# Row vectors sent as lines, tables written by halves, and a first norm centred ahead of the ranks, in a two-layer graph attention kernel

## The chip, the cores and the metric

The kernel runs on one core of a Trainium2 chip. The metric is the device time of one execution in microseconds, the median of three runs. Before the change it is 2462.87 us (2462.56 to 2469.74); the profiled execution took 2464.5 us.

The engines are named as in the profile: PE is the matrix engine (TensorE), PEld its weight loads, DVE is VectorE, ACT is ScalarE, POOL is GpSimd, and SP is SyncE, which issues most DMA transfers. "POOLq" and "SPq" are the instruction queues of GpSimd and SyncE.

## What is computed

The input is x, 16 batches of 1024 nodes with 256 features, and one adjacency matrix of 1024 x 1024. Two residual layers follow one another, all in fp32:

```
# layer 0
h   = relu(layernorm(x))
r   = relu(h @ mlp1_w + b1)                     # 1024 x 512
a   = elu(gat(r, None, W_fc, a_fc))             # dense attention, slope 0.2
o   = elu(a) + r
r2  = relu(o @ mlp2_w + b2)                     # 1024 x 256
b   = elu(gat(r2, adj, W_hand, a_hand))         # masked attention, slope 0.2
x   = x + relu(elu(b) + r2)
# layer 1
h   = relu(layernorm(x))
g   = h @ W
x   = x + relu(softmax(mask(leaky(e_src + e_dst, 0.01))) @ g)   # masked by adj

def gat(inp, adj, W, a):
    h = inp @ W;  f1 = h @ a[:F];  f2 = h @ a[F:]
    e = leaky_relu(f1[:, None] + f2[None, :]);  mask by adj if given
    return elu(softmax(e) @ h)
```

## The kernel before

The work of one batch is spread over two and more steps of a software pipeline. In one step, which lasts some 147 us, the kernel does the masked attention of layer 0 of batch b, the masked attention of layer 1 of the batch before, the dense attention of batch b + 1 or b + 2, and the first norm of a batch still later. The names are: `Norm` (layer norm and transposition to features by nodes), `Dense` (first MLP, dense attention, second MLP), `Gnn0` and `Gnn1` (masked attentions; `Masked` is their base).

**The dense attention is not done as a 1024 x 1024 product.** leaky_relu makes the weight of a pair one of two products, according to the sign of f1 + f2. So the nodes are sorted by f2, running sums over the sorted rows are kept from both ends, and each node looks up the two sums at its own threshold. The steps are:

- `project` (L453) makes h on PE, with f1 and f2 as extra columns; ACT copies it to SBUF as `hnat`.
- `columns` (L468) gathers f2 of the 8 tiles in `fs` on DVE. `send` (L473) writes these 1024 numbers to DRAM (`row_r`), through the helper `send_row` (L240); `row` (L476) reads them back, broadcast to 128 partitions (`r`, 512 KB).
- `rank` (L501) counts, for a tile of 128 nodes, how many nodes come before each, in 3 or 4 passes of DVE over the broadcast row. `sign` (L540) counts on ACT against the other threshold.
- `scatter` (L518) writes the rows of a tile to their sorted place in DRAM by an indirect DMA; `read_sorted` (L555) reads the sorted rows back as `xs`, 8 consecutive rows to a partition, in two halves.
- `sums_weights` (L584) makes `bd` on ACT; `sum_before` (L591) makes the running sums `tt` from the front, and `sum_behind` (L608) those from the end, in place in `xs`, on DVE. `write_table` (L599) writes `tt` and `xs` to the table `fine` in DRAM, 2 MB each. `carry` (L617) makes the sums between partitions on PE and writes them to the table `coarse`.
- `gather` (L628) reads, for each tile, one row of `fine`, and adds one of `coarse`, by indirect DMA on GpSimd. `share`, `mean`, `merge` and `merge_end` (L643 to L719) put the result together, transpose it (`hpT` on PE) and add it to `resT`; `mlp2` (L721) follows.

**The first norm** of a batch (`first_norm`, L774) takes statistics (L258, L259 on DVE), a root on GpSimd (L263, L264), centres (L268 on DVE, `hn`) and transposes on PE (L278, `nt`), four tiles at a time; ACT applies the relu (L282, `hT`). It does this for half 0 and, some 20 us later, for half 1.

**The masked attention of layer 1** needs a row of weights broadcast as well (`rowsb`). It goes the same way, through `send_row`, as `row_b` and back (L349 to L360).

**The order of work is written out by hand.** `at(lo, hi, steps)` puts steps in a table with a time in us, and at the end the table is sorted and emitted in that order. For PE, DVE, ACT and SP this order is the order of instructions on the engine, and GpSimd is chained to it likewise, apart from the scatters, which are free among themselves. The times only sort: each engine works its queue in order and waits for what an instruction needs. `t0` is the start of a step; a period is written as 142.

A transfer on SP waits for its data at the head of SP's queue. The tiles of x come from one pool of three buffers with the tag `x`: `load_first` (L753) fetches x for the first norm, `load_again` (L756) fetches it once more for the residual sums.

The change touches `send_row` and its two callers, `write_table`, and the times of `first_norm`, `dense_begin` (L798), `dense_sums` (L813), `load_again` in `masked_first` (L863), `m.send` in `second_norm` (L902), `load_first` (L1022), and the table writes of the written-out start (L960, L962, L992, L994).

Of the kernel before, what the change touches and what calls it, by code (L numbers as in the profile page):

```python
# [8 lines left out]
F32 = mybir.dt.float32  # L9
# [8 lines left out]
P = 128  # L18
# [13 lines left out]
def fast_path(ctx: ExitStack, tc: tile.TileContext, alarm, x, adj, w1, b1, w2, b2, w_fc, a_fc,  # L32
# [21 lines left out]
    nc = tc.nc  # L54
    NB, N, F = x.shape
    H = w1.shape[1]
    NT = N // P
# [5 lines left out]
    K = H + 1  # L63
# [3 lines left out]
    work = ctx.enter_context(tc.tile_pool(name="work", bufs=2))  # L67
# [10 lines left out]
    def bc_psum(name):  # L78
        return psum.tile([P, NH * HALF], F32, tag="bc", name=name, bufs=1)
# [11 lines left out]
    ident = const.tile([P, P], F32, name="ident")  # L91
# [90 lines left out]
    row_d = {s: [dram.tile([1, N], F32, name=f"row_{s}{k}") for k in range(2)] for s in "rb"}  # L182
# [39 lines left out]
    def at(lo, hi, steps):  # L222
        for i, step in enumerate(steps):
            table.append((lo + (hi - lo) * i / len(steps), len(table), step))
# [12 lines left out]
        for u in range(len(col)):  # L237
            nc.tensor.transpose(dst[:, u * P:(u + 1) * P], col[u].to_broadcast([P, P]), ident)

    def send_row(dst, col):  # L240

        nc.sync.dma_start(dst.rearrange("o (u i) -> i (o u)", i=P), col)

    class Norm:

# [46 lines left out]
    def half(h):  # L292
        return slice(h * TH, (h + 1) * TH)
# [4 lines left out]
    class Masked:  # L298
# [48 lines left out]
            nc.vector.tensor_scalar_max(qwd[:, 2, :], qwd[:, 2, :], D_MIN)  # L347

        def send(self):  # L349
            send_row(row_d["b"][self.b % 2], self.qwd[:, 0, :])  # L350

        def row(self, sent=False):

# [74 lines left out]
    class Dense:  # L428
# [42 lines left out]
            nc.vector.tensor_reduce(self.ext, self.fs[:, 1, :], AX.X, OP.max)  # L471

        def send(self):  # L473
            send_row(row_d["r"][self.b % 2], self.fs[:, 1, :])

        def row(self, sent=False):  # L476

# [77 lines left out]
        def read_sorted(self):  # L555

            if self.split:
                self.xs = [big.tile([P, TH, R], F32, tag=tag, name=f"xs_{self.b}_{h}", bufs=bufs)
                           for h, (tag, bufs) in enumerate((("onat", 1), ("x", 3)))]
            else:  # L560
                xs = big.tile([P, NT, R], F32, tag="seq", name=f"xs_{self.b}", bufs=2)
                self.xs = [xs[:, half(h), :] for h in range(2)]
                self.xs_all = xs
            rows = sorted_d[self.b % 2].rearrange("(p r) f -> p r f", p=P)
            for h in range(2):
                reader = nc.sync.dma_start(self.xs[h], rows[:, half(h)])
                for made in self.writers:
                    wait_for(reader, made, "rows of the buffer")
                self.readers.append(reader)

        def sums_begin(self):
            b = self.b
            self.bd = small.tile([P, 2, NT], F32, tag="bd", name=f"bd_{b}")
            if self.split:
                self.tt = [big.tile([P, TH, K], F32, tag="hm", name=f"tt_{b}_{h}", bufs=2)
                           for h in range(2)]
            else:
                tt = big.tile([P, NT, K], F32, tag="seq", name=f"tt_{b}", bufs=2)
                self.tt = [tt[:, half(h), :] for h in range(2)]
                self.tt_all = tt  # L580
            self.all_t = work.tile([P, K], F32, tag="part", name=f"all_{b}")
            nc.gpsimd.memset(self.tt[0][:, 0, :], 0.0)

# [12 lines left out]
            else:  # L596
                nc.vector.scalar_tensor_tensor(tt[r + 1], row, bd, tt[r], op0=OP.mult, op1=OP.add)

        def write_table(self, s):  # L599

            dst = fine_d[self.b % 2][:N, s * K:(s + 1) * K].rearrange("(p r) f -> p r f", p=P)
            if self.split:
                for h, part in enumerate(self.xs if s else self.tt):
                    nc.sync.dma_start(dst[:, half(h)], part[:, :, :K])
            else:
                nc.sync.dma_start(dst, self.xs_all[:, :, :K] if s else self.tt_all)

        def sum_behind(self, r):  # L608
            rows = [self.xs[u // TH][:, u % TH, :K] for u in range(NT)]
# [140 lines left out]
    xs = {}  # L750
# [17 lines left out]
    def each(f, *ranges):  # L768
        out = [()]
        for r in ranges:  # L770
            out = [o + (i,) for o in out for i in r]
        return [partial(f, *o) for o in out]

    def first_norm(t0, b):  # L774

        n = norm1[b]
        lo = t0 - (62 if b == 2 else 29.5)
        at(lo, lo + 1, n.stats_steps(0))
        at(t0 - 13, t0 - 9, n.stats_steps(1))
        n.turn_at(t0 - (14.5 if b == 2 else 22), 0, 4)  # L780
        n.turn_at(t0 + 0.2, 1, 4)

    def mlp_steps(b):
# [13 lines left out]

    def dense_begin(t0, b):  # L798
        d = dense[b]
        at(t0 - 38.5, t0 - 38.5, [d.columns, d.send, partial(d.row, True)])  # L800
        at(t0 - 31.5, t0 - 31.5, [d.highest])
        at(t0 - 28, t0 - 12, each(d.rank, range(NT)))
        at(t0 - 33, t0 - 30.5, [partial(d.project, t, 0) for t in range(2)])
        at(t0 - 21, t0 - 8, [partial(d.project, t, 0) for t in range(2, NT)])
        scatters(d, t0 - 18.5, t0 - 4.5)
        at(t0 - 6, t0 - 6, [d.query])
        at(t0 - 4, t0 - 4, [d.read_sorted])
# [5 lines left out]
    def dense_sums(t0, b):  # L813
        d = dense[b]
        at(t0 - 3, t0 - 3, [d.sums_begin])
        at(t0 - 22, t0 - 4, each(d.sign, range(NT)))
        for h in range(2):
            at(t0 + 6.5 + 4 * h, t0 + 6.5 + 4 * h, [partial(d.sums_weights, h)])
            at(t0 + 7.5 + 5 * h, t0 + 12.5 + 5 * h, each(d.sum_before, tiles(h)))
        at(t0 + 18, t0 + 18, [partial(d.write_table, 0)])  # L820
        at(t0 + 18, t0 + 32, each(d.sum_behind, range(NT - 1, -1, -1)))
        at(t0 + 32, t0 + 32, [partial(d.write_table, 1)])
        at(t0 + 33, t0 + 33, [d.count])
        at(t0 + 50.5, t0 + 50.5, each(d.carry, range(2)))

# [31 lines left out]
    def masked_first(t0, b):  # L857
        m, n = gnn0[b], norm2[b]
        at(t0 + 1, t0 + 1, [m.vectors])
        at(t0 + 4, t0 + 4, [m.row])  # L860
        at(t0 + 4.5, t0 + 10, each(m.scale, range(NT)))
        weights(m, 0, t0 + 5.5, t0 + 10)
        at(t0 + 3, t0 + 3, [partial(load_again, b)])  # L863
        at(t0 + 4.5, t0 + 11, each(dense[b].natural, range(NT // 2)))
        at(t0 + 11, t0 + 39, each(m.product, range(NQ), range(NT)))
        for q in range(1, NQ):
            weights(m, q, t0 + 5.5 + 7 * q, t0 + 12 + 7 * q)
        for t in range(NT):
            lo = t0 + 18.2 + 7 * (t // 2) + 0.6 * (t % 2)
            at(lo, lo, [partial(m.finish, t)])  # L870
            at(lo + 1.2, lo + 1.2, [lambda t=t: m.combine(t, dense[b].o_nat)])
            at(lo + 5.2, lo + 5.2, [lambda t=t: m.update(t, xs[b])])
            at(lo + (6.2 if last(b) or b == 0 else 9), lo + (6.2 if last(b) or b == 0 else 9), [partial(n.stats, t)])
        at(t0 + 36, t0 + 36, [partial(n.root, 0)])
        lo = t0 + (46.5 if last(b) or b == 0 else 51)
        at(lo, lo, [partial(n.root, 1)])
# [4 lines left out]
    def second_norm(t0, b):  # L881
        n, m = norm2[b], gnn1[b]
        if last(b):
            n.turn_at(t0 + 46.5, 0)
            n.turn_at(t0 + 49, 1, 1.6)
            lo = t0 + 50
        elif b == 0:
            n.turn_at(t0 + 47, 0)
            n.turn_at(t0 + 50.5, 1, 1.6)
            lo = t0 + 47.2  # L890
        else:
            n.turn_at(t0 + 53.3, 0)
            n.turn_at(t0 + 67.3, 1)
            lo = t0 + 71
        at(lo, lo + 7, each(m.project, range(NT)))
        at(lo + 7.5, lo + 7.5, [m.extremes])
        if last(b, 2):
            at(lo + 7.8, lo + 7.8, [m.vectors])
            at(lo + 8.2, lo + 8.2, [m.row])
            at(lo + 8.3, lo + 9.5, each(m.scale, range(NT)))  # L900
        else:
            at(lo + 11, lo + 11, [m.vectors, m.send])  # L902
            at(lo + 40, lo + 52, each(m.scale, range(NT)))
            at(base_of(b + 1) + 22, base_of(b + 1) + 22, [partial(m.row, True)])

# [51 lines left out]
    for h in range(2):  # L957
        at(START + 82 + 3 * h, START + 82 + 3 * h, [partial(d.sums_weights, h)])
        at(START + 83 + 4 * h, START + 87 + 4 * h, each(d.sum_before, tiles(h)))
    at(START + 91, START + 91, [partial(d.write_table, 0)])  # L960
    at(START + 91, START + 98, each(d.sum_behind, range(NT - 1, -1, -1)))
    at(START + 98, START + 98, [partial(d.write_table, 1)])  # L962
    at(START + 98, START + 98, [d.count])
    at(START + 100, START + 100, each(d.carry, range(2)))
    for t in range(TH):
# [23 lines left out]
    for h in range(2):  # L989
        at(START + 150 + 3 * h, START + 150 + 3 * h, [partial(e.sums_weights, h)])  # L990
        at(START + 151 + 5 * h, START + 156 + 5 * h, each(e.sum_before, tiles(h)))
    at(START + 161, START + 161, [partial(e.write_table, 0)])  # L992
    at(START + 161, START + 175, each(e.sum_behind, range(NT - 1, -1, -1)))
    at(START + 175, START + 175, [partial(e.write_table, 1)])  # L994
    at(START + 175, START + 175, [e.count])
    at(START + 180, START + 180, each(e.carry, range(2)))
    for b in range(NB):
# [21 lines left out]
            dense_rows(after_base - PERIOD, b + 2)  # L1019
            dense_begin(after_base, b + 2)  # L1020
        if b + 3 < NB:
            lo = after_base - PERIOD + 73  # L1022
            at(lo, lo, [partial(load_first, b + 3)])
            first_norm(after_base, b + 3)

# [464 lines left out]
```

## Time and profile before

| engine | busy us | share of the span |
|---|---|---|
| PE | 2305.0 | 94% |
| PEld (beside PE) | 1779.3 | 72% |
| DVE | 1635.6 | 66% |
| ACT | 1252.3 | 51% |
| POOL | 967.2 | 39% |

The page gives busy time of each engine, groups of instructions with the idle time ahead of them, and what ended that idle time. A group's line is read from the left: line of the kernel, engine, operation, what it writes and reads, shape, count; then busy us and mean ns; then us of idle time of that engine just ahead of it, with the releaser. The timeline lists an engine's instructions in order of time: start, length, engine, line, operation, and in brackets the idle time ahead. The chain of waits goes from the last instruction backwards to what released it; a piece of it with "DMA" is a transfer on which the next instruction waited.

DMA moves 348.41 MB in the span, 141 GB/s on the average. By tenths of the span's slices its engines are busy from 2 to 8, so it comes in bursts. In the stretch from 1000 to 1150 us its share of busy time is 1.01 to 1.07 from 1110 to 1140 us and 0.01 from 1000 to 1010 us.

### The profile page before, as it was taken

To read this page: it belongs to the slowest core of one execution; us is meant where nothing else is said; L and a number is where in the kernel's file an instruction comes from. 1 tells how busy PE (TensorE), PEld (TensorE's weight loads), DVE (VectorE), ACT (ScalarE), POOL (GpSimd) and SP (SyncE) were. 2 spreads that over 40 slices of the span, in tenths; PEclk is the share of its full clock that TensorE was granted. 3 is DMA by queue.
4 is the path that set the end of the run, shared out by engine and by line. 5 is a ranking of instruction groups with operands and counts; after the bars stand their busy time and mean duration, and the time that the engine had idled before them with its cause. 6 is when DMAs were issued, how large, how long until landed. Compare 5 with 4: busy or idle time off the path is not lost.

```text
span 2464.5 us, 30883 instructions
## 1 busy us (share of the span) xinstructions
PE 2305.0 (94%) x10025; PEld 1779.3 (72%) x10025; DVE 1635.6 (66%) x4499; ACT 1252.3 (51%) x2712; POOL 967.2 (39%) x1216
## 2 busy tenths in 40 slices
PE   8988899998999999999899989989999999999897
PEld 6666677776867768677776867767676786877666
DVE  6765684765847567684765857567684865858554
ACT  4355645546455553645546355553645546364442
POOL 1153344253433526344353523526344353533320
PEclk9999999999999999999999999999999999999899
DMA  4558266482645728256482645638266482736600
GB/s 171 154 161 203 52 163 159 137 213 68 191 103 158 185 100 206 76 165 158 136 214 93 176 92 163 180 112 201 74 177 148 129 214 94 187 87 165 161 1 28
DMA packets 176714, 348.41 MB, mean 141 GB/s; under 512 B 39192, under 2 KB 90392, under 8 KB 172448
## 3 DMA queue, kind: packets, MB, share of 16 engines
q1 hardware_dynamic: 130592, 182.36, 27.7%
q0 software_dynamic: 45952, 163.99, 24.7%
q8 instruction: 82, 1.34, 0.3%
q14 instruction: 88, 0.72, 0.1%
HBM read 220.06 MB, written 126.24 MB: 141 GB/s over the span
## 4 chain that ended last, share of the span: by engine, by line
PE 57%; DVE 20%; DMA 13%; ACT 4%; POOL 3%; issue 2%; DVEq 0%; POOLq 0%; ACTq 0%; SPq 0%
PE h L461 16%; PE oa L380 9%; PE ob L380 7%; PE m L447 7%; DMA row_r<-fs 6%; PE pa L318 4%; DVE attb L369 4%; DVE atta L369 4%; PE pb L318 3%; DMA got<-coarse,k 3%; POOL got L637 3%; PE m L726 3%; DMA r<-row_r 3%; PE nt L278 3%; DVE xs L614 2%
## 5 line engine op out<-in xcount | busy, mean ns | idle before, releaser
L461 PE MATMUL h<-wfc_sb,resT 128*128 128x257 f32 x2048 | 477.8, 388 | 0.0
L380 PE MATMUL oa<-hma,atta 128*128 128x258 f32 x2048 | 457.4, 383 | 11.4 <-DVE atta L369 11.4
L380 PE MATMUL ob<-hmb,attb 128*128 128x257 f32 x2048 | 456.5, 382 | 5.5 <-DVE attb L369 5.5
L380 PEld LDWEIGHTS oa<-hma,atta 128*128 128x128 f32 x2048 | 385.6, 190 | 78.3 <-DVE atta L369 22.8
L380 PEld LDWEIGHTS ob<-hmb,attb 128*128 128x128 f32 x2048 | 389.9, 191 | 61.0 <-ACT hmb L364 3.7
L461 PEld LDWEIGHTS h<-wfc_sb,resT 128*128 128x128 f32 x2048 | 391.0, 195 | 56.1 <-issue 1.0
L719 POOL TENSOR_TENSOR resT<-resT,e 128x512 f32<-128x512 f32 x128 | 163.1, 1274 | 410.7 <-DVE e L718 365.6
L369 DVE SCALAR_TENSOR_TENSOR atta<-rowsa,qwda,edge 128x256 f32<-128x256 f32 x512 | 263.3, 542 | 47.3 <-ACT rowsa L360 33.0
L404 POOL TENSOR_TENSOR posa<-posa,onat 128x256 f32<-128x256 f32 x120 | 106.7, 889 | 437.8 <-ACT posa L396 437.8
L369 DVE SCALAR_TENSOR_TENSOR attb<-rowsb,qwdb,edge 128x256 f32<-128x256 f32 x512 | 256.6, 530 | 29.1 <-PE ob L380 26.4
L447 PE MATMUL m<-hT,w_sb 128*128 128x512 f32 x512 | 235.8, 598 | 0.5 <-ACT posa L396 0.5
L726 PE MATMUL m<-resT,w_sb 128*128 128x512 f32 x512 | 230.3, 596 | 4.4 <-POOL resT L719 4.4
L395 ACT ACTIVATE ea<-oa,reca 128x256 f32<-128x256 f32 x128 | 60.8, 475 | 330.5 <-DVE reca L392 304.3
L637 POOL DMA_INDIRECT got<-coarse,k x124 | 194.6, 1569 | 38.1 <-issue 36.9
L418 ACT ACTIVATE rb<-ob,recb 128x256 f32<-128x256 f32 x128 | 57.5, 474 | 267.0 <-DVE recb L416 267.0
L278 PE MATMUL nt<-ident,hn 128*128 128x128 f32 x512 | 86.9, 318 | 101.1 <-DVE hn L268 98.0
L710 DVE TENSOR_SCALAR e<-hpT 128x512 f32<-128x512 f32 x128 | 88.3, 690 | 139.9 <-PE hpT L708 135.3
L726 PEld LDWEIGHTS m<-resT,w_sb 128*128 128x128 f32 x512 | 93.9, 191 | 106.9 <-issue 94.1
L637 POOL DMA_INDIRECT got<-fine,k x124 | 129.7, 1046 | 78.8 <-DVE ea L405 35.6
L278 PEld LDWEIGHTS nt<-ident,hn 128*128 128x128 f32 x512 | 69.4, 162 | 124.5 <-issue 89.8
L509 DVE TENSOR_SCALAR_CACHE_REDUCE junk<-r,fs 128x1024 uint8<-128x1024 f32 (+7 forms) x128 | 103.5, 809 | 83.4 <-DMA r<-row_r 82.6
L447 PEld LDWEIGHTS m<-hT,w_sb 128*128 128x128 f32 x512 | 92.6, 193 | 88.8 <-issue 86.1
(177 smaller groups left out, 3592.7 us busy)
## 6 DMA issues: line engine op xcount, KB each, us to landing
xs<-sorted SPq DMA_DIRECT2D x32, 1028.0 KB
fine<-tt SPq DMA_DIRECT2D x15, 2052.0 KB
fine<-xs SPq DMA_DIRECT2D x15, 2052.0 KB
x<-in_x_dram SPq DMA_DIRECT2D x16, 1024.0 KB
out_dram<-x SPq DMA_DIRECT2D x32, 512.0 KB
xn<-in_x_dram SPq DMA_DIRECT2D x15, 1024.0 KB
coarse<-carry SPq DMA_DIRECT2D x32, 256.5 KB
r<-row_r SPq DMA_DIRECT2D x14, 512.0 KB
```

The lines of the kernel that those rows point to most:

```text
L278: nc.tensor.transpose(self.ps[c][:, u * P:(u + 1) * P], self.hn[t][:, c * P:(c + 1) * P], ident)
L318: nc.tensor.matmul(ps[:, :2 + F], lhsT=hT[:, c, t * P:(t + 1) * P], rhs=self.w_sb[:, c, 0, :], start=(c == 0), stop=(c == FC - 1))
L369: nc.vector.scalar_tensor_tensor(a_t, self.rows[:, q * PAIR:(q + 1) * PAIR], self.qwd[:, 1, j:j + 1], edge[:, j, q * PAIR:(q + 1) * PAIR], ...
L380: nc.tensor.matmul(self.out[t][:, :F + self.ONES], lhsT=self.att[q, j][:, (t % 2) * P:(t % 2 + 1) * P], rhs=self.hm[:, j, 2:2 + F + self.O ...
L404: adder.tensor_add(pos, pos, o_nat[:, t, :])
L447: nc.tensor.matmul(ps, lhsT=w1_sb[:, kc, c * P:(c + 1) * P], rhs=hT[:, kc, h * HALF:(h + 1) * HALF], start=(kc == 0), stop=(kc == FC - 1))
L461: nc.tensor.matmul(ps[:, :F + 1], lhsT=self.resT[:, kc, t * P:(t + 1) * P], rhs=wfc_sb[:, kc, g, :], start=(kc == 0), stop=(kc == HC - 1))
L509: nc.vector.tensor_scalar(junk[:, t * P:], r2[:, t * P:], s, None, op0=OP.is_lt, op1=OP.add, accum_out=rank[:, 1, t:t + 1])
L637: nc.gpsimd.indirect_dma_start(out=got[u // n][:, u % n, :], out_offset=None, in_=(coarse_d if coarse else fine_d)[self.b % 2][:, :], in_o ...
L710: nc.vector.tensor_scalar_min(e, ps, 0.0)
L719: nc.gpsimd.tensor_add(dst, dst, e)
L726: nc.tensor.matmul(ps, lhsT=w2_sb[:, kc, c * P:(c + 1) * P], rhs=self.resT[:, kc, h * HALF:(h + 1) * HALF], start=(kc == 0), stop=(kc == H ...
```

## The change

It has five parts.

1. A row of 1024 numbers, which lies in SBUF as 128 partitions x 8, is transposed on PE to 8 partitions x 128 and copied by ACT to a tile `line`, and goes to DRAM as 8 lines of 128 numbers. Before, the DMA wrote it as 1024 single numbers. The column copy keeps its time, the send comes 1.7 later in the table; the send of the weights of layer 1 comes 13 later.
2. In the steps from the fourth batch on, the statistics of the first norm come 4 earlier in the table and its first centring 3 earlier, which puts the statistics ahead of `highest` and three of four centrings ahead of the first rank. The fourth comes after it.
3. The tables `fine` are written in two halves each, and each half as soon as its sums are there: the sums from the front write half 0 first, the sums from the end half 1 first.
4. `load_again` comes 7 later and `load_first` 13 later in the table, meant to keep them out of the way of rows and gathers.
5. The start is changed accordingly.

```diff
-    def send_row(dst, col):
-
-        nc.sync.dma_start(dst.rearrange("o (u i) -> i (o u)", i=P), col)
+    def send_row(dst, col, name):
+
+        ps = bc_psum(f"{name}_ps")
+        nc.tensor.transpose(ps[:NT, :P], col, ident)
+        line = work.tile([NT, P], F32, tag="carry", name=name, bufs=2)
+        nc.scalar.copy(line, ps[:NT, :P])
+        nc.sync.dma_start(dst.rearrange("o (u i) -> (o u) i", i=P), line)
...
-        def write_table(self, s):
+        def write_table(self, s, h):
 
             dst = fine_d[self.b % 2][:N, s * K:(s + 1) * K].rearrange("(p r) f -> p r f", p=P)
-            if self.split:
-                for h, part in enumerate(self.xs if s else self.tt):
-                    nc.sync.dma_start(dst[:, half(h)], part[:, :, :K])
-            else:
-                nc.sync.dma_start(dst, self.xs_all[:, :, :K] if s else self.tt_all)
+            nc.sync.dma_start(dst[:, half(h)], (self.xs if s else self.tt)[h][:, :, :K])
...
     def first_norm(t0, b):
 
         n = norm1[b]
-        lo = t0 - (62 if b == 2 else 29.5)
+        lo = t0 - (62 if b == 2 else 33.5)
         at(lo, lo + 1, n.stats_steps(0))
         at(t0 - 13, t0 - 9, n.stats_steps(1))
-        n.turn_at(t0 - (14.5 if b == 2 else 22), 0, 4)
+        n.turn_at(t0 - (14.5 if b == 2 else 22), 0, 4 if b == 2 else 7)
         n.turn_at(t0 + 0.2, 1, 4)
...
-        at(t0 - 38.5, t0 - 38.5, [d.columns, d.send, partial(d.row, True)])
+        at(t0 - 38.5, t0 - 38.5, [d.columns])
+        at(t0 - 36.8, t0 - 36.8, [d.send, partial(d.row, True)])
...
-        at(t0 + 18, t0 + 18, [partial(d.write_table, 0)])
+        at(t0 + 13, t0 + 13, [partial(d.write_table, 0, 0)])
+        at(t0 + 18, t0 + 18, [partial(d.write_table, 0, 1)])
         at(t0 + 18, t0 + 32, each(d.sum_behind, range(NT - 1, -1, -1)))
-        at(t0 + 32, t0 + 32, [partial(d.write_table, 1)])
+        at(t0 + 25, t0 + 25, [partial(d.write_table, 1, 1)])
+        at(t0 + 32, t0 + 32, [partial(d.write_table, 1, 0)])
...
-        at(t0 + 3, t0 + 3, [partial(load_again, b)])
+        at(t0 + 10, t0 + 10, [partial(load_again, b)])
...
-            at(lo + 11, lo + 11, [m.vectors, m.send])
+            at(lo + 11, lo + 11, [m.vectors])
+            at(lo + 24, lo + 24, [m.send])
...
-    at(START + 98, START + 98, [partial(d.write_table, 1)])
+    at(START + 98, START + 98, each(d.write_table, [1], (1, 0)))
...
-    at(START + 175, START + 175, [partial(e.write_table, 1)])
+    at(START + 168, START + 168, [partial(e.write_table, 1, 1)])
+    at(START + 175, START + 175, [partial(e.write_table, 1, 0)])
...
-            lo = after_base - PERIOD + 73
+            lo = after_base - PERIOD + 86
             at(lo, lo, [partial(load_first, b + 3)])
```

## The prediction

> **What bounds the kernel now.** I read the page's busy shares first: PE is busy 94% of the span, DVE 66%, so the question is where PE's missing 6% lies. The list of waits gives one large answer, and the costliest groups say the same on two lines:
>
> ```profile
> L278 PE MATMUL nt<-ident,hn 128*128 128x128 f32 x512 | 86.9, 318 | 101.1 <-DVE hn L268 98.0
> ...
> L509 DVE TENSOR_SCALAR_CACHE_REDUCE junk<-r,fs 128x1024 uint8<-128x1024 f32 (+7 forms) x128 | 103.5, 809 | 83.4 <-DMA r<-row_r 82.6
> ```
>
> The reader is to see that PE stood still 98 us ahead of the transposes of the first norm, all released by the centring on DVE, and that DVE stood still about as long for the broadcast row. PE's timeline shows that it is one hole per batch. From 1000 to 1150 us:
>
> ```profile
> 1017.25 7.03 PE L726 MATMUL m<-resT,w_sb 128*128 128x512 f32 x16
> 1030.27 1.94 PE L278 MATMUL nt<-ident,hn 128*128 128x128 f32 x8 [6.00 <-DVE hn L268]
> 1032.01 11.24 PE L461 MATMUL h<-wfc_sb,resT 128*128 128x257 f32 x48
> ...
> 1050.06 1.03 PE L278 MATMUL nt<-ident,hn 128*128 128x128 f32 x8
> ```
>
> Thirteen such holes (first at 290 us, last at 2061 us) are 5.6 to 6.8 us long and sum to 78.9 us, 6.07 each; outside them PE is nearly gapless. A batch takes 147.6 us (twelve from 290.5 to 2061.2 us). Last, the chain of waits says what fills the hole:
>
> ```profile
> 1010.76 0.60 DVE e L718
> 1011.46 10.69 DMA row_r<-fs
> 1022.16 3.62 DMA r<-row_r
> 1025.81 1.30 DVE junk L509 x2
> ...
> 1029.80 0.34 DVE hn L268
> 1030.27 1.94 PE nt L278 x8
> ```
>
> The row write of 4 KB takes 10.69 us, the broadcast read of 512 KB 3.62 us. DVE then ranks tiles 0 and 1 before it centres, so a row that the centring does not need holds PE. DVE's statistics were over at 1020.1 and GpSimd's root at 1021.6 us.
>
> [...] after the hole 8 transposes take 1.94 us, elsewhere 0.87 in the chain, and the granted clock is 0.83 from 1020 to 1040 us, 1.00 in the other stretches. [...] This row goes out as 1,024 packets of 4 B[...]. [...] landings of the single 2 KB zero rows here, on SyncE's queue, come 1.75 to 1.8 us after issue.
>
> **The change, part by part.**
>
> (1) Centring ahead of ranks. Statistics move ahead of `highest`, and three of four centrings ahead of rank 0; the fourth comes after rank 0 alone. Statistics follow `merge_end` (ends 1016.8) and take 4 x 0.535: 1018.9. GpSimd's root, 1.3 us with its start: 1020.4. Three centrings of 0.34: 1021.5. PE wants them at 1024.3, where it now falls idle. So they are no longer late.
>
> (2) Row by lines. The send becomes a PE transpose to 8x128, a ScalarE copy, and 8 packets of 512 B. PE pays one pass of 0.11 us (8 nt transposes take 0.87), twice a batch: +0.22. The copy stands behind the last exponential of `merge` (ends 1016.05); its cost lies between ScalarE's 128x8 operations (0.21) and 128x257 copies (0.37), say 0.25, and lies in ScalarE's slack. Issue at 1016.3, against 1011.46: the send itself starts later. Its landing is the unknown. Lower bound 1.75 (a zero row), upper 4.7 us (slowest landing of a scatter of 128 rows); I take 1.9, since there are 8 packets and an idle queue: before, no data packet runs from 1005 until the row's. Then 3.62 for the read: the row is there at 1021.8 instead of 1025.81, 4.0 earlier. Rank 0 (1.93) and the fourth centring (0.34) end at 1024.1; PE wants it at 1025.05, the fourth pair of transposes. The first hole closes.
>
> New waits: on PE, behind the new transpose are the projections; it waits for DVE's column copy, over at 1011.4, long before PE comes at 1013.7. On ScalarE the copies wait for the buffers of earlier carries, whose writes land over 30 us before.
>
> (3) What then comes next. With the hole gone PE reaches the second group of transposes at 1024.4 + 0.87 + 10.4 + 6.97 = 1042.65. Their centring waits for all ranks: row + 1.93 + 0.34 + 7 x 1.98 = +16.1, then 3.71 (in the timeline from rank 7's end to the centring: statistics and root), then 4 x 0.345: row + 21.3 with its semaphore, 1043.1 for the last. PE needs that at 1042.65 + 0.65 = 1043.3. So this wait just closes too: 0 to 0.3 us, I take 0.2. It has no reserve; each us by which the row is later stands here.
>
> The ranks also set the scatters and the reload of the sorted rows: last rank 4 us earlier, so its issue moves from 1052.55 to about 1048.2; its halves landed 5.1 and 7.6 us after issue, so 1053.3 and 1055.8. ScalarE wants them (`bd`, 1060.77 and 1064.3 now, where the chain is on PE) 7 us earlier, 1053.8 and 1057.3. Reserve 0.5 us: costs nothing, but barely.
>
> (4) Tables by halves. Same bytes, two issues of 0.4 us more on SyncE, which idles. The behind table now is issued whole at 1086.61 and lands at 1101.48; GpSimd waits 1.04 us for it. With half of it away by 1078 the rest lands near 1095, so gathers start 0.85 us earlier. That matters as reserve: gathered rows land at 1131.3 and 1143.2, DVE finishes them at 1136.1 and 1149.9, and PE takes them at 1136.07 and 1149.97. Some batches (148.7 us against 146.7) wait a little there: 6.2 us in the list of waits. I count 3 us for the run.
>
> (5) Loads of x. Compared queue by queue, SyncE's order changes only in batch 0, where x goes behind the behind table. In the other batches these loads stand where they stood, and cost and bring nothing. In batch 0 the table landed 26.7 us after its issue and held the gathers until 215.2; PE lost 4.47 us at 235.5 to the root queued behind those gathers. Without the load ahead this shrinks; but x, landed at 199.6, now comes near its first use at 208.9. Between 0 and 6 us, I take 3.
>
> (6) The last batch with a rank has no hole but small PE waits from 2220 to 2230 us (2.16 + 0.76 + 0.89 + 0.62 + 0.72), behind a ScalarE that started its sign passes with the late row. 2 to 3 us of 5.2 go.
>
> The sum for a batch: hole 6.07, half clock after it 1.07 in the transposes and 0.68 in the projections (11.24 against 10.56 us in the batch at 2201 us, which has no hole), less 0.22, less 0.2: 7.4. Thirteen times: 96. With 3 + 3 + 2.5: about 104 us off 2462.9, near **2360 us**.
>
> **Rivals.** *The row stays late (B).* For: the landing of 8 packets in this form is not in the trace. At the upper bound, 4.7, the row comes at 1024.6: the fourth centring is 1.95 late, the later group 0.65 more, and a hole of that size can still cost the half clock (a wait of 2.16 at 2220 us did), so 7.6 - 2.6 - 1.7 = 3.3 a batch, with 5 elsewhere: 2415. Against: an idle queue and the zero rows.
>
> *The chain of sums and gathers takes over (C).* Rank, scatter, sorted rows, sums, tables, gathers and means touch PE with no reserve at 1136 and 1150. They gain only the row's 4 us and 0.85, while PE would gain 7.4; if the reserves of (3) are not real, a batch shortens by 4: 13 x 4 = 52, 2411. Against: from `bd` on, each link waits for work that PE itself released, and moves with it.
>
> *Slower (D).* In-order queues get 28 new transposes and 28 new copies, 30 more DMA issues; DMA is saturated (share 1.0) from 1110 to 1140. If the hole reappears whole at the second group and each new step costs 0.5 us of PE, 2462.9 + 14 = 2477. Against: none of the named waits is late.
>
> **How the numbers follow.** A 0.76 at 2360, B 0.10 at 2415, C 0.09 at 2411, D 0.05 at 2477. Within A, a landing from 1.75 to 3 us and the unknown ends of (4) to (6) give 2345 to 2385. I reach to 2398 for the near ends of B and C. Faster by over 0.3% is A, B and C but for 0.02; slower is 0.04.
>
> **What would show it.** Right: no wait of nt for hn in the thirteen batches, a clock near 0.99, row write near 2 us, ranks starting 4 us sooner after `merge_end`, batches near 140.2 us. Wrong: a hole ahead of the second group or the masked products (row or sorted rows late), or waits of hpT for hp (C).

## The result, and the profile after

The changed kernel takes 2359.11 us (median of four, 2358.27 to 2360.0); the kernel before, in the same comparison, 2463.41. The ratio is 0.9571, with a 95% interval from 0.9555 to 0.9588: some 104 us, or 4.3%, are gone. 2360 was predicted.

The page of the kernel after, its first line of busy times and its chain of waits by engine:

```profile
PE 2281.2 (97%) x10053; PEld 1759.2 (75%) x10053; DVE 1637.7 (69%) x4499; ACT 1250.3 (53%) x2740; POOL 968.0 (41%) x1216
...
PE 21%; DVE 9%; ACT 2%; issue 1%; POOL 0%; DMA 0%; DVEq 0%; ACTq 0%; POOLq 0%
```

PE's share goes from 94% to 97%. Its busy time fell by 23.8 us, though it got 28 more transposes: 12.0 us in the transposes `nt` and 11.8 in the projections `h`, for the most part work which no longer runs at half clock: in the eight transposes behind each of the thirteen holes the granted clock was 0.50, in the same transposes it is 1.00 now (over the span 0.971 before, 0.991 now). The chain could be followed back over the last third of the span only; in it DMA, which had 13% of the chain before, has 0%.

The two groups that carried the prediction, now at lines L282 and L513, in the list of all groups (busy us, mean ns, then the idle time ahead of them with its releasers):

```profile
L513 DVE TENSOR_SCALAR_CACHE_REDUCE junk<-r,fs 128x1024 uint8<-128x1024 f32 (+7 forms) x128 | 103.3, 807 | 4.9 <-DMA r<-row_r 4.1 <-ACT r L488 0.8
...
L282 PE MATMUL nt<-ident,hn 128*128 128x128 f32 x512 | 74.9, 285 | 18.7 <-DVE hn L272 15.5 <-ACT rb L422 2.6 <-ACT hT L286 0.5
```

PE's wait for the centring went from 98.0 to 15.5 us, and what is left lies at the start (9.9 us ahead of the first transposes of all) and at the end. DVE's wait for the row went from 82.6 to 4.1 us. PE's timeline around the same place of a batch:

```profile
970.36 0.27 PE L243 MATMUL line_ps<-ident,fs 128*8 128x128 f32 x1
...
974.04 7.03 PE L724 MATMUL m<-resT,w_sb 128*128 128x512 f32 x16
980.91 1.04 PE L282 MATMUL nt<-ident,hn 128*128 128x128 f32 x8
981.78 10.57 PE L465 MATMUL h<-wfc_sb,resT 128*128 128x257 f32 x48
...
999.59 1.03 PE L282 MATMUL nt<-ident,hn 128*128 128x128 f32 x8
```

There are no brackets: neither group of transposes waits. The eight transposes take 1.04 us instead of 1.94, the projections 10.57 instead of up to 12.5. In all thirteen batches the hole is zero.

SyncE's two transfers of the row in that batch, and DVE's centring and first rank:

```profile
972.91 0.28 SPq L246 DMA_DIRECT2D row_r<-line  x1
974.13 0.35 SPq L484 DMA_DIRECT2D r<-row_r  x1
```

```profile
977.09 1.09 DVE L272 TENSOR_SCALAR hn<-xn,mv,rstd 128x256 f32<-128x256 f32 x3 [1.07 <-POOL rstd L268]
978.11 1.27 DVE L513 TENSOR_SCALAR_CACHE_REDUCE junk<-r,fs 128x1024 uint8<-128x1024 f32 x1
...
980.03 0.41 DVE L272 TENSOR_SCALAR hn<-xn,mv,rstd 128x256 f32<-128x256 f32 x1
```

The read is issued when the write has landed, so the write took 1.22 us; over the run the reads wait 13.8 us for the fourteen writes at SyncE's queue, 131.4 before. The row is at hand before DVE has centred three tiles: the first rank follows without a wait. DVE now waits only for GpSimd's root.

**Where the time came from.** I compare the start of the same PE instructions in the two profiles, whose spans differ by 106.2 us. At the end of the first hole (290.48 before, 281.23 after) the gain is 9.25; by that of the last one (2061.21 and 1959.86) it is 101.35. So twelve batches give 92.1 us, or 7.68 each. Behind the last hole come 0.6 more up to 2190 us (its half clock, granted clock 0.50 in its transposes, less small losses), then 3.5 in the last batch with a rank, which has no hole, and 0.85 in the tail. Of the first 9.25, 5.8 are the first hole, and 3.5 lie ahead of it; where these come from is taken up with the loads of x below.

### The profile page after: what moved, and what is told of

The parts are those of the page before. It is cut to its first block, busy times and chain, and to the rows that moved or that the text cites. A ratio compares the mean times of both kernels' runs of the same rounds, so it can differ in the third digit from the quotient of the medians.

```text
span 2358.3 us, 31110 instructions
## 1 busy us (share of the span) xinstructions
PE 2281.2 (97%) x10053; PEld 1759.2 (75%) x10053; DVE 1637.7 (69%) x4499; ACT 1250.3 (53%) x2740; POOL 968.0 (41%) x1216
## 5 line engine op out<-in xcount | busy, mean ns | idle before, releaser
L384 PE MATMUL oa<-hma,atta 128*128 128x258 f32 x2048 | 457.7, 384 | 12.5 <-DVE atta L373 12.5
L465 PE MATMUL h<-wfc_sb,resT 128*128 128x257 f32 x2048 | 466.0, 380 | 0.0
L465 PEld LDWEIGHTS h<-wfc_sb,resT 128*128 128x128 f32 x2048 | 378.9, 190 | 53.5 <-issue 1.0
L548 ACT ACTIVATE junk<-r,fs 128x1024 int8<-128x1024 f32 x124 | 142.7, 1151 | 12.4 <-POOL fs L469 12.1
L525 POOL DMA_INDIRECT sorted<-hnat,place x128 | 131.4, 1027 | 39.5 <-issue 15.3
L709 ACT ACTIVATE e<-e 128x512 f32<-128x512 f32 x128 | 80.7, 630 | 91.2 <-DVE e L708 91.0
```

Of the source, the lines that this page charges most:

```text
L384: nc.tensor.matmul(self.out[t][:, :F + self.ONES], lhsT=self.att[q, j][:, (t % 2) * P:(t % 2 + 1) * P], rhs=self.hm[:, j, 2:2 + F + self.O ...
L465: nc.tensor.matmul(ps[:, :F + 1], lhsT=self.resT[:, kc, t * P:(t + 1) * P], rhs=wfc_sb[:, kc, g, :], start=(kc == 0), stop=(kc == HC - 1))
L525: made = nc.gpsimd.indirect_dma_start(out=sorted_d[self.b % 2], out_offset=bass.IndirectOffsetOnAxis(ap=self.place[:, t:t + 1], axis=0), i ...
L548: nc.scalar.activation(junk, self.r2, AF.Sign, bias=self.fs[:, 0, t:t + 1], accum_out=self.signs[:, t:t + 1])
L709: nc.scalar.activation(e, e, AF.Exp)
```

## The experiments

My theory was that one path only, the row (written, read back, ranked against) and the centring queued behind it, set all thirteen holes, and that parts 3 and 4 of the change are worth a few us at most. The rivals were that one of parts 1 and 2 does everything alone, that it is the filling of PE's idle time or the clock that counts, and that the new kernel stands on the edge of a next wait. All ten runs that follow are compared with the kernel before on the same chip, in three comparisons: the first has the four kernels from centring to both, the second the changed kernel again, tables, loads and statistics, the third the hops. The kernel before took 2452.7, 2463.7 and 2474.6 us in them, while the kernels that have no hole and no new wait stayed within 2359.1 and 2361.6. So a ratio holds within its comparison; kernels without the old row write are best set beside the 2359.86 us of the changed one.

| run | what it is | us | ratio (95%) | hole, mean us |
|---|---|---|---|---|
| after, again | the changed kernel | 2359.86 | 0.9576 (0.9561 to 0.9591) | 0 |
| centring | before + part 2 alone | 2414.94 | 0.9840 (0.9815 to 0.9865) | 2.95 |
| lines | before + part 1 alone | 2376.03 | 0.9682 (0.9655 to 0.9708) | 1.16 |
| filler | before + idle products | 2435.91 | 0.9922 (0.9892 to 0.9951) | 0.55 beside the filler |
| both | before + parts 1 and 2 | 2361.63 | 0.9625 (0.9605 to 0.9644) | 0 |
| tables | after without part 3 | 2360.84 | 0.9589 (0.9567 to 0.9611) | 0 |
| loads | after without part 4 | 2360.32 | 0.9580 (0.9563 to 0.9596) | 0 |
| one hop | after + one more copy of the row | 2371.19 | 0.9595 (0.9565 to 0.9624) | 0.47 |
| two hops | after + two more copies | 2412.39 | 0.9748 (0.9722 to 0.9774) | 2.49 |
| statistics | after, second norm's statistics later | 2376.51 | 0.9649 (0.9633 to 0.9665) | 0 |

For the changed kernel run again, which is there for comparison, this was expected:

> The changed kernel once more, to stand on the same chip as the three runs beside it. Every theory: 2359 us as before, within 0.3%.

### Centring ahead alone

```diff
-        lo = t0 - (62 if b == 2 else 29.5)
+        lo = t0 - (62 if b == 2 else 33.5)
...
-        n.turn_at(t0 - (14.5 if b == 2 else 22), 0, 4)
+        n.turn_at(t0 - (14.5 if b == 2 else 22), 0, 4 if b == 2 else 7)
```

> The kernel before with part 2 of the change alone (statistics and three centrings ahead of the ranks); the row still goes out as 1024 single numbers. Theory (the row itself is the delay, the order on DVE only part of it): the row still arrives 1025.8 in the batch shown, so the fourth centring, behind rank 0, ends at 1028.1 where PE wants it at 1025.05: a hole of 3 us stays ahead of its transposes, and 0.8 us ahead of the second group, with the half clock after it. Gain 2 to 3 us a batch: 2425 to 2437 us. Rival (the order on DVE was the whole fault, the row is hidden once it is out of the way): 2365 us.

Measured: 2414.94 us, below the theory's band and far from the rival's 2365. The band was worked out from 2463 us; at this ratio that gives 2424, still just below it. The wait of 0.8 us that was expected ahead of the second group did not come in any batch. Its chain of waits in one batch, and PE's timeline there:

```profile
982.04 0.60 DVE e L718
982.74 10.51 DMA row_r<-fs
993.26 3.42 DMA r<-row_r
996.71 1.30 DVE junk L509 x2
...
998.72 0.34 DVE hn L268
999.11 0.69 PE nt L278 x2
```

```profile
995.39 0.82 PE L278 MATMUL nt<-ident,hn 128*128 128x128 f32 x6
999.11 0.69 PE L278 MATMUL nt<-ident,hn 128*128 128x128 f32 x2 [2.90 <-DVE hn L268]
999.59 13.36 PE L461 MATMUL h<-wfc_sb,resT 128*128 128x257 f32 x48
```

Six transposes run at once and the last two wait 2.90 us for the fourth centring, which stands behind rank 0 and so behind the row. The hole is halved, not closed. And in this batch the projections take 13.36 us, with a granted clock of 0.83 from 1000 to 1015 us, longer than any in the kernel before (11.1 to 12.5): here a hole of half the length still cost the clock. It did so in nine of the thirteen batches, and the projections of the whole run take 479.9 us, against 466.0 in the changed kernel.

### Lines alone

```diff
-        nc.sync.dma_start(dst.rearrange("o (u i) -> i (o u)", i=P), col)
+        ps = bc_psum(f"{name}_ps")
+        nc.tensor.transpose(ps[:NT, :P], col, ident)
+        line = work.tile([NT, P], F32, tag="carry", name=name, bufs=2)
+        nc.scalar.copy(line, ps[:NT, :P])
+        nc.sync.dma_start(dst.rearrange("o (u i) -> (o u) i", i=P), line)
...
-        at(t0 - 38.5, t0 - 38.5, [d.columns, d.send, partial(d.row, True)])
+        at(t0 - 38.5, t0 - 38.5, [d.columns])
+        at(t0 - 36.8, t0 - 36.8, [d.send, partial(d.row, True)])
```

> The kernel before with part 1 of the change alone (rows go out as 8 lines); the order on DVE stays. Theory: the row arrives 5 us sooner (in the profile after, written in 1.2 us and read in 3.3), ranks 0 and 1 and the four centrings end 5 us sooner, which leaves a hole of about 1 us, too short for the half clock: gain 6.5 us a batch, 2372 to 2380 us. Rival (both parts are needed, since the centring still stands behind a row that PE has not asked for): a hole of over 2 us with the half clock, gain under 4 us a batch, over 2410 us.

Measured: 2376.03 us, in the theory's band. The hole is there still, but short, and the projections behind it take 10.56 us, as in the changed kernel (466.0 us over the run in both; granted clock 0.990 over the span):

```profile
987.15 1.32 PE L282 MATMUL nt<-ident,hn 128*128 128x128 f32 x8 [1.05 <-DVE hn L272]
988.30 10.56 PE L465 MATMUL h<-wfc_sb,resT 128*128 128x257 f32 x48
```

So part 1 is the larger part (some 77 us of 91 in this comparison), and part 2 takes away the remaining 1.16 us a batch. The weights of layer 1 go by lines too in this kernel. That was not tried apart, but PE's wait of `ob` for the weights made from them is 5.5 us in all with and without.

### Filling the hole with products

Six products that nobody reads are put ahead of the first norm's transposes of each batch from the fourth on (twelve records in the trace), and nothing else is changed.

```diff
+    def keep_busy(b):
+        ps = bc_psum(f"busy_{b}")
+        for i in range(BUSY):
+            nc.tensor.matmul(ps[:, :HALF], lhsT=ident, rhs=w1_sb[:, 0, :], start=True, stop=True)
...
+        if b > 2:
+            at(t0 - 22.05, t0 - 22.05, [partial(keep_busy, b)])
```

> The kernel before with six products of 128x512 on PE in the hole of each of the thirteen batches (5.2 us of PE work on constants, the result is not used). The row, the ranks and the centring come no sooner. Theory (the half clock after an idle hole is a cost of its own, 1.07 us in the transposes and 0.68 in the projections): PE idles only about 1 us, the clock stays at 1.00 and each batch is 1.7 us shorter: 2438 to 2443 us. Rival (the slow transposes and projections are slow for another reason, such as late operands): no change, 2463 us.

Measured: 2435.91 us, ratio 0.9922, so 19 us less (12 to 26), where the theory's 1.7 us a batch make 22. PE's timeline:

```profile
1006.51 5.31 PE L778 MATMUL busy<-w_sb,ident 128*128 128x512 f32 x12
1012.28 1.32 PE L278 MATMUL nt<-ident,hn 128*128 128x128 f32 x8 [0.46 <-DVE hn L268]
1013.44 10.57 PE L461 MATMUL h<-wfc_sb,resT 128*128 128x257 f32 x48
```

The row is as late as ever, and yet the projections are back at 10.57 us (granted clock 0.988 over the span). That measures the clock's part by itself: 19 us over 13 holes are 1.5 us for each (0.9 to 2.0). From the two traces it is 1.6: the projections after a hole take 11.58 us in the mean before, 1.01 over 10.57, and the transposes 1.94, where they take 1.32 here. (Those 1.32 are still more than the 1.04 of the changed kernel, since here each pair of transposes follows its centring, one after the other.) The rest of each hole is the wait itself, and no filler brings that back.

### Both, without parts 3 and 4

This kernel is the one before with the diffs of the centring and of the lines; part 5 is left out with parts 3 and 4.

> The kernel before with parts 1 and 2 alone; tables whole, loads of x where they were. Theory (they carry nearly all): thirteen holes with their half clock, 7.5 a batch, and 4 us in the last batch with a rank: 2360 to 2366 us. Rival (tables by halves keep the gathers from becoming the bound once the hole is gone): waits of hpT for hp in most batches and 2375 us or more.

Measured: 2361.63 us, no hole in any batch; 1.8 us beside the changed kernel's 2359.86, 0.08%. Parts 1 and 2 are the whole gain. They are not independent: by the ratios part 1 alone brings 3.2%, part 2 alone 1.6%, both 3.75%. On top of part 1, part 2 is worth 14.4 us (2376.03 - 2361.63), and 13 holes of 1.16 us are 15.1. On top of part 2, part 1 is worth 53.3, and 13 times (2.95 of hole + 1.2 of slowed projections + 0.3 of slower transposes - 0.22 of new transposes) are 55.0. Each sum fits to 2 us because the hole is one wait: what one part leaves over the other takes.

### Tables whole again

The edit is shown for the steps of the pipeline; in the written-out start the tables are whole again as well.

```diff
-        at(t0 + 13, t0 + 13, [partial(d.write_table, 0, 0)])
-        at(t0 + 18, t0 + 18, [partial(d.write_table, 0, 1)])
+        at(t0 + 18, t0 + 18, [partial(d.write_table, 0)])
...
-        at(t0 + 25, t0 + 25, [partial(d.write_table, 1, 1)])
-        at(t0 + 32, t0 + 32, [partial(d.write_table, 1, 0)])
+        at(t0 + 32, t0 + 32, [partial(d.write_table, 1)])
```

> The changed kernel with its tables written whole again, as before the change (part 3 undone). Theory (only reserve for the gathers): GpSimd waits about 1 us for the table in each batch, PE meets the gathered rows where it did; 0 to 5 us more than the changed kernel, 2359 to 2364 us. Rival (the gathers become the bound once the hole is gone): waits of hpT for hp of 1 us and more in most batches, 2370 us or more.

Measured: 2360.84 us, against 2359.86 with the halves: no difference that can be told (the runs of this kernel span 2355 to 2366). GpSimd's timeline at the first gather of a batch, in this kernel and then in the changed one:

```profile
1053.18 1.29 POOL L641 DMA_INDIRECT got<-fine,k  x1 [0.29 <-DMA fine<-xs]
```

```profile
1050.58 1.25 POOL L635 DMA_INDIRECT got<-fine,k  x1 [0.33 <-issue]
```

In this batch the wait for the table that the halves remove is no more than the 0.3 us that stand ahead of the gather in the changed kernel too. Over the whole run GpSimd waits for the table five times with whole tables, 4.1 us in all and 1.3 at most. And nothing that PE waits for hangs on it: PE's wait of `hpT` for `hp` is 6.2 us before, 6.4 after, 6.4 here.

### Loads of x as before

```diff
-        at(t0 + 10, t0 + 10, [partial(load_again, b)])
+        at(t0 + 3, t0 + 3, [partial(load_again, b)])
...
-            lo = after_base - PERIOD + 86
+            lo = after_base - PERIOD + 73
```

> The changed kernel with both loads of x at their former times (part 4 undone). SyncE's order then differs in the first batch alone, where the load of x again stands ahead of the second table. Theory: 0 to 4 us more than the changed kernel, all of it in the first batch, through a later start of its gathers. Rival (the loads had got in the way of rows and gathers in every batch): 10 us more.

Measured: 2360.32 us, no difference. The hole of 4.47 us at 235.5 us, which the prediction put down to these loads, is not there either. PE's timeline in this kernel, and in the one with lines alone, which has the old loads and the old tables:

```profile
232.00 0.76 PE L282 MATMUL nt<-ident,hn 128*128 128x128 f32 x4 [0.44 <-DVE hn L272]
```

```profile
231.61 0.76 PE L282 MATMUL nt<-ident,hn 128*128 128x128 f32 x4 [0.44 <-DVE hn L272]
```

The runs with centring alone, with the filler and with both parts have the old loads as well, and no gap over 0.9 us there; the filler's kernel does the very same as the kernel before up to that place. So that hole was seen in the one profiled execution of the kernel before alone, in which the gathers of batch 0 began at 215.2 us instead of 210 to 211. Why they did then stays open. The 3.5 us ahead of the first hole are no gain of the change.

### One and two more hops of the row

To see what reserve the changed kernel has, the row is copied once, or twice, more from DRAM to DRAM before it is broadcast. The edit is shown for one hop; the other kernel has `range(2)`.

```diff
-                nc.sync.dma_start(self.r2, row_d["r"][self.b % 2].to_broadcast([P, N]))
+                src = row_d["r"][self.b % 2]
+                for k in range(1):
+                    hop = hop_d[k][self.b % 2]
+                    nc.sync.dma_start(hop.rearrange("o (u i) -> (o u) i", i=P),
+                                      src.rearrange("o (u i) -> (o u) i", i=P))
+                    src = hop
+                nc.sync.dma_start(self.r2, src.to_broadcast([P, N]))
```

> The changed kernel with the row of the ranks copied once more within DRAM ahead of the broadcast, which makes it late by one small transfer, 1.3 to 2.2 us. Theory (there is a reserve now, read from the profile after: the row arrives 0.7 us before DVE asks for it, and the second group of centrings ends 0.75 us before PE needs it): the first 1.4 us are free, so 0 to 0.8 us of waiting a batch: 2359 to 2370 us. Rival of the prediction (no reserve, each us stands before the second group): 1.3 to 2.2 us a batch, 2376 to 2388 us.

> The same with two copies within DRAM, the row late by 2.6 to 4.4 us. Theory (reserve 1.4 us, then one for one[...]): 1.2 to 3 us of waiting a batch and up to 1.7 us of half clock: 2375 to 2415 us, the wait first ahead of the first group of transposes, then of the second. Rival (no reserve): 2.6 to 4.4 us and half clock, 2410 to 2440 us.

Measured: 2371.19 us, 1.2 above the theory's band and below the rival's, and 2412.39 us, in the band. One hop makes the row 1.9 us later (6.71 us from issue to row in the median, 4.83 without), two hops 4.0 (8.81). With one hop, the batch in which the row was latest shows this on PE:

```profile
987.29 0.44 PE L283 MATMUL nt<-ident,hn 128*128 128x128 f32 x2 [1.71 <-DVE hn L273]
987.56 10.56 PE L466 MATMUL h<-wfc_sb,resT 128*128 128x257 f32 x48
...
1005.76 1.04 PE L283 MATMUL nt<-ident,hn 128*128 128x128 f32 x8
```

In the other batches PE waits from 0 to 1.2 us. The cost, 11.3 us beside 2359.86, is one of small waits: 6.3 us more for `hn` (21.8 against 15.5 in the list of waits) and 3.1 more of `pa` for ScalarE. After the wait of 1.71 us the projections still take 10.56, and 466.0 over the run, as in the changed kernel (granted clock 0.993 over the span). With two hops, SyncE's queue and then PE's timeline in one batch:

```profile
991.46 0.29 SPq L247 DMA_DIRECT2D row_r<-line  x1
993.81 0.47 SPq L488 DMA_DIRECT2D hop<-row_r  x1
995.75 0.47 SPq L488 DMA_DIRECT2D hop<-hop  x1
997.59 0.36 SPq L491 DMA_DIRECT2D r<-hop  x1
```

```profile
1003.73 0.69 PE L283 MATMUL nt<-ident,hn 128*128 128x128 f32 x2 [3.45 <-DVE hn L273]
1004.21 11.98 PE L466 MATMUL h<-wfc_sb,resT 128*128 128x257 f32 x48
...
1023.00 1.04 PE L283 MATMUL nt<-ident,hn 128*128 128x128 f32 x8
```

A hole is back, and after it the projections are slowed by the clock in ten of the thirteen batches: 11.98 us here, with a granted clock of 0.87 from 1004 to 1016 us, and 481.2 over the run. In both kernels it is the first group of transposes that waits, by its fourth pair; the second, 18 us later, never does.

### Statistics of the second norm later

This was to gain more: `oa` waits 12.5 us in all for `atta` on DVE, in two waits of some 0.6 and 0.25 us a batch, with statistics of the second norm among the work ahead of it.

```diff
-            at(lo + (6.2 if last(b) or b == 0 else 9), lo + (6.2 if last(b) or b == 0 else 9), [partial(n.stats, t)])
-        at(t0 + 36, t0 + 36, [partial(n.root, 0)])
-        lo = t0 + (46.5 if last(b) or b == 0 else 51)
+            at(lo + (6.2 if last(b) or b == 0 else 13), lo + (6.2 if last(b) or b == 0 else 13), [partial(n.stats, t)])
+        lo = t0 + (36 if last(b) or b == 0 else 39.5)
+        at(lo, lo, [partial(n.root, 0)])
+        lo = t0 + (46.5 if last(b) or b == 0 else 53.2)
```

> The changed kernel with the statistics of the second norm 4 later in the table, and its two roots 3.5 and 2.2 later. In the profile after, PE waits 0.6 and 0.2 us a batch for weights on DVE that stand behind these statistics. Theory (the order on DVE makes these waits): they go, 0.6 us in each of 13 batches, 2350 to 2353 us. Rival (DVE is full there, so that the wait only moves to a later product or to the second norm): within 0.2% of the changed kernel.

Measured: 2376.51 us, 16.6 slower than the changed kernel: a miss. The list of PE's waits:

```profile
PE carry L620 <- ACT rb L422: 15.2, 14, 1.1
PE oa L384 <- DVE atta L373: 7.3, 13, 0.7
```

and DVE's and PE's timelines in one batch:

```profile
918.20 0.42 DVE L262 BATCH_NORM_STATS2 stats<-x 128x6 f32<-128x256 f32 x1
918.65 0.18 DVE L263 BATCH_NORM_AGGREGATE mv<-stats 128x2 f32<-128x6 f32 x1
918.75 0.20 DVE L420 RECIPROCAL recb<-ob 128x1 f32<-128x1 f32 x2
```

```profile
919.53 1.14 PE L620 MATMUL carry<-all,upto 128*128 128x257 f32 x4 [1.08 <-ACT rb L422]
```

The wait of `oa` fell by 5 us, but the statistics now stand ahead of the reciprocal `recb`. ScalarE's `rb` waits for that, and PE's `carry` for `rb`, which still holds its PSUM buffer: a new wait of 1.08 us in each of 14 batches, 15.2 in all, in the list where the changed kernel has none. The products `ob` ahead of it come slower as well, since their weights stand behind statistics on DVE: 56 of them take 13.04 us in this batch, 12.30 in the changed kernel. No version tried beats the changed kernel.

## Why the prediction was right

The mechanism was right: the late row, and the centring queued behind it, made the thirteen holes, and parts 1 and 2 closed them. That the time is met to 1 us is luck: two terms of the sum were wrong, and others that came out larger made up for most of them.

**The row path is one straight line.** For each batch the traces give L, the time from the issue of the row's write to the landing of its broadcast, and the hole that follows. In every batch with a hole but one (of 62), hole = L minus a constant, to 0.02 us. L is read from the issue times on SyncE's queue and the landings in the trace:

| kernel | L, median us | constant | hole |
|---|---|---|---|
| before | 14.26 | 8.32 | 5.6 to 6.8 |
| centring alone | 13.82 | 11.05 | 2.5 to 3.7 |
| lines alone | 4.85 | 3.67 | 0.9 to 1.6 |
| one hop | 6.71 | 6.40 | 0 to 1.7 |
| two hops | 8.81 | 6.40 | 1.9 to 3.5 |
| after | 4.83 | 6.40 | 0 |

Centring ahead adds 2.7 us to the constant, in both pairs (11.05 - 8.32, 6.40 - 3.67). Sending by lines takes 4.65 from it, since the write is issued that much later, and 9.0 to 9.4 from L. The last row is the changed kernel: a reserve of 1.57 us in the median, 0.4 in its slowest batch (5.96).

**By the prediction's steps.**

1. Centring ahead: right. DVE waits for the root, 1.07 us, and no longer for the row.
2. The row by lines: right in kind; the later issue (4.84 predicted, 4.65 measured) and the copy (0.25; 0.24) are right in size. The write was mis-sized: 1.9 us were taken, with 1.75 as lower bound; it takes 1.23 in the median. The bound came from the landing of single 2 KB rows, 1.75 to 1.8 us. So the row came 4.8 us earlier (14.26 - 4.83 - 4.65), not 4.0.
3. What comes next: wrong on the safe side. The second group was to wait 0.2 us, without reserve, and each later us to stand there. It does not wait at all, and with the row 4 us later it still does not: the first group's fourth pair stops PE before, and that shifts the second group along. Reserve is at the first group. The sorted rows landed at 1008.92 and 1011.44 us in one batch, `bd` took them at 1010.30 and 1013.82: a reserve of 1.4 us, not 0.5.
4. The tables by halves: wrong. The gathers did lose their wait for the table (1.04 us in the batch read, 0.3 now), but with whole tables it is 0.29 too, so the halves did not do it, and the 3 us counted for the run are zero. They came from the 6.2 us that `hpT` waits for `hp`. Those waits lie ahead of 252 us and behind 2220 us, in both profiles, and in no batch between; they were never the table's.
5. The loads of x: the 3 us were wrong in their cause. They look right in the profiles (3.5 us), which compare one disturbed start of before with an undisturbed one; the experiment says zero.
6. The last batch with a rank: 3.5 us, 2.5 predicted. The small waits fell from 5.15 to 2.87 us, as forecast; the rest is half clock after the wait of 2.16 us (granted clock 0.50 from 2223 to 2226 us), which is gone too.

For a batch 7.4 us were predicted, 7.68 came. The hole is 6.06; the transposes and projections after it lost 1.9 (1.75 predicted, from a batch whose projections take 11.24; their mean is 11.58); less 0.22 for the new transposes that makes 7.74. By the filler some 1.6 of the 1.9 are the clock, and the rest is the pace at which the centring feeds the transposes. The 0.2 of waiting at the second group did not come; in its place PE now waits 0.16 to 0.55 us a batch for `hma` ahead of `pa`, 3.5 us in all.

Over the run the thirteen holes gave 98.5 us in the two profiles (5.8, 92.1 and 0.6), where 96 were predicted, step 6 gave 3.5 and the tail 0.85, which was not in the sum. That is 102.8, against 104 predicted, of which the 6 us of steps 4 and 5 are not there. The medians differ by 104.3; the 1.5 us between lie within the scatter, since the kernel before alone ran from 2462.56 to 2469.74.

**The rivals.** B, the late row, is real as a mechanism: two hops, with 5.0 us from the write's issue to the read's, are near that case (4.7 there): 2412 us, where 2415 was worked out. It did not come, since the write took 1.23. C, the sums and gathers taking over, is shut out by batches of 139.9 us, in which `hpT` does not wait for `hp` once. D, the hole whole again at the second group, needs a wait that no run showed.

## What to carry to other kernels

When a wait is set by a path of several steps, measure the path's length batch by batch and set it against the hole: if the slope is one, the constant is the slack, and each part of a change can be priced on it apart. A gap seen once in one profile is no gain to count on; look for it in a second execution first. And before an operation is moved to later on a busy engine that works its queue in order, look at what then stands behind it: here a statistics of 0.5 us held a reciprocal, a copy and a buffer of PE, at 1.08 us a batch.

## What the runs showed of the hardware

- 4 KB as 1,024 packets of 4 B took 8.7 to 11.4 us from the issue of the write to the issue of the read that waits for it; as 8 lines of 512 B 1.2 to 1.5 us (once 2.65), on the same queue in the same stretch of the batch, in 14 rows each. Why the first form takes longer was not shown.
- The kernel before also differed by up to 22 us from one comparison to the next, and kernels with lines and no hole by 2.5. That the old row write makes the difference is my estimate, from the holes and the clock: only with it does the row set the end, by its own length or by the half clock behind its holes (granted clock 0.970 to 0.976 in the fastest of the three comparisons, 0.967 to 0.970 in the slowest). It was not measured apart.
- In these runs a hole ahead of the first norm's transposes cost clock when it was long, and none when it was short. In the 13 batches of before, with holes of 5.6 to 6.8 us, the granted clock is 0.50 in the transposes after each, and the projections take 11.1 to 12.5 us instead of 10.57. In the 39 batches of after, lines and one hop, with holes up to 1.71 us, no projections are slowed: 466.0 us over the run in each of the three. Of the 26 batches with holes of 1.9 to 3.7 us (centring, two hops) 19 have slowed projections; over the two runs all projections come to 479.9 and 481.2 us, against 477.8 in the kernel before. The loss does not grow with the length: the projections took 13.36 us after a hole of 2.90, 11.98 after 3.45 and 11.24 after 6.00. So a hole of 3 us can cost as much clock as one of 6. What decides between 1.9 and 3.7 us was not shown.
- A copy of the 4 KB row from DRAM to DRAM, in 8 lines, added 1.9 to 2.1 us to the path in the median.
